# The last pairs of three graph layers in a drain of their own, in a four-layer graph network on one core

## The chip, the core and the metric

The kernel runs on one core of one Trainium2 chip. The metric is the device time of one execution in microseconds, lower is better; all matrix work is in fp32.

## The reference, cut to what matters

The input `x` holds 32 graphs of 512 nodes with 64 features; `adj` is one normalised 512 x 512 adjacency for all of them. Four layers follow each other, each with a layer norm before it and a residual around it:

```python
h = relu(layernorm(x)); x = x + (h @ w_self + adj @ h @ w_nbr + bias)      # layer 0
h = relu(layernorm(x)); z = h
for i in range(2): z = relu((adj @ z) @ weights[i])
x = x + z                                                                  # layer 1
h = relu(layernorm(x)); Wh = h @ W.T
e = leaky_relu(Wh @ a[:64] [:, None] + Wh @ a[64:] [None, :], 0.2)
x = x + elu(softmax(where(adj > 0, e, -9e15)) @ Wh)                        # layer 2
h = relu(layernorm(x)); ...                                                # layer 3
```

Layer 3 ("flow") is an attention over the graph with 8 heads of 128 features, followed by an output attention; its scores are products of the node features with themselves.

## The kernel before, in words

Graphs are worked on in pairs, 16 in all (`M`), two graphs side by side in 128 features. The first three layers form one software pipeline of slots: in slot `k`, `slot(k, more)` issues layer 0 of pair `k`, the norm of layer 1 for pair `k - 1`, the first half of layer 1 for pair `k - 2`, its second half for `k - 3`, and of layer 2 the preparation of pair `k - 4` and the attention of pair `k - 5`. There are `M + 5` slots, 0 to 20; in the last ones ever less of the pipeline is left. The order on TensorE, VectorE and ScalarE is the order in which the code issues, written out by hand; the queues of the engines are fed in that order, and a framework puts in the semaphores.

Layer 2 of a pair is an object of class `Gat`. Its steps, with the line numbers of the profile before:

- `flip` transposes the normed pair on TensorE and copies it on ScalarE (L290, L292).
- `prepare` computes the projected features `wh_ps` (L878) and one score vector `e1` (L885) on TensorE, then exponentials of the two score vectors on ScalarE (L894 to L897).
- `weigh` multiplies the features by those exponentials on VectorE (L902).
- `scores(part)` builds four of eight mask products `s` on VectorE (L911). A row of the softmax is the maximum of two exponentials times the mask.
- `values` multiplies the mask products by the weighted features on TensorE: 64 matmuls (128 records) into two PSUM accumulators `acc` (L924). The pool of accumulators holds one pair.
- `end` divides by the softmax sum on VectorE (L935, L936), which reads the accumulators; takes an exponential on ScalarE (L941); adds both parts to `x` (L944, L945); and centres the result and squares it for the norm of layer 3 (L773 to L775, L947).

`Norm.a` centres a pair (L773 to L775), `Norm.square` squares it on ScalarE, `Spread` sums variances (L811), takes the root on ScalarE (L818) and the reciprocal on VectorE (L826), and `Norm.relu` scales (L797). `neighbours` is a product with the adjacency (four matmuls, L833) and `project` one with a weight (L852).

`more` is one extra piece of work in a slot, issued after the slot's last neighbour product and ahead of `u.end()`. In slots 16 to 19 it is `judge_rows(c)` (L195 to L204), which checks a quarter of the adjacency's rows on VectorE; in slot 20 it is `judge` (L221 to L225), which reduces the checks to one flag: a reduction on VectorE, a transpose `own_ps` on TensorE, and two small VectorE steps on that. The flag is used at the end of the whole kernel.

In slot 19 pair 14 is `u` and pair 15 is `last`; both are ended there. Slot 20 takes the variances of what is left.

The flow stage follows under `planned`, which issues units of work by a fixed table of offsets. Its lead-in, `flow_slot(i)` for `i` from -12 to -2, is issued after slot 17. It makes the first graph's flow features: a norm on VectorE (L474 to L478), a scaling on GpSimd (`hs`, L483), a transpose on TensorE (`hx_ps`, L290), a copy, and the products `g_ps` (L508). The first scores `s_ps` (L386) and their VectorE step (L372) come after the pipeline has ended. SBUF buffers rotate: the pool `work_a` has two buffers of each name, `row_pair` 11 in all, `ps_a` four PSUM banks under one tag.

Of the kernel before, what the change touches and what calls it, by code (L numbers as in the profile page):

```python
# [8 lines left out]
F32 = mybir.dt.float32  # L9
AF = mybir.ActivationFunctionType  # L10
# [12 lines left out]
def fast_form(  # L23
# [731 lines left out]
    with (  # L755
# [105 lines left out]
        class Gat:  # L861
# [51 lines left out]
                        mask_t[b // C][:, b % C], op0=OP.max, op1=OP.mult,  # L913
                    )

            def values(self):

                self.acc = [
                    ps_g.tile([P, C, F + 1], F32, name="acc") for k in range(2)
                ]  # L920
                for r in range(C):
                    for b in range(2 * C):
                        for k in range(2):
                            nc.tensor.matmul(  # L924
                                self.acc[k][:, r],
                                lhsT=self.s[b // 2][halves(k), b % 2, r * P : (r + 1) * P],
                                rhs=self.v[halves(k), b],
                                start=(b == 0), stop=(b == 2 * C - 1),
                            )

            def end(self):
                rec = tiny.tile([P, 2, C], F32, name="rec")
                self.sq = o = work.tile([P, 2, C, F], F32, name="o")
                for k in range(2):
                    nc.vector.reciprocal(rec[:, k], self.acc[k][:, :, F])  # L935
                    nc.vector.tensor_tensor(  # L936
                        o[:, k], self.acc[k][:, :, :F],
                        rec[:, k, :, None].to_broadcast([P, C, F]), OP.mult,
                    )
                e = row_pair("e")[:, 0].rearrange("p (k c f) -> p k c f", k=2, c=C)  # L940
                nc.scalar.activation(e, o, AF.Exp)  # L941

                x4 = pair_of(self.i)
                nc.vector.scalar_tensor_tensor(x4, o, 0.0, x4, op0=OP.max, op1=OP.add)  # L944
                nc.vector.scalar_tensor_tensor(x4, e, 1.0, x4, op0=OP.min, op1=OP.add)  # L945
                self.mean = centre(o, self.i)
                nc.scalar.activation(o, o, AF.Square)  # L947
                ended.append(self)
# [12 lines left out]
        def start():  # L961
# [8 lines left out]
            order_adj()  # L970
            transpose_adj(ps_t)

        def slot(k, more):
# [25 lines left out]
            u = gat.pop(k - 5, None)  # L999
            if u:  # L1000
                u.scores(0)
            if k - 3 in nt1b:

                po = project([(nt1b.pop(k - 3), wl2[1])], "po1b")
                x4 = pair_of(k - 3)
                for i in range(2):
                    nc.vector.scalar_tensor_tensor(
                        x4[:, i], po[:, :, i, :], 0.0, x4[:, i], op0=OP.max, op1=OP.add
                    )
# [12 lines left out]
            if k - 4 in gat:  # L1022
                gat[k - 4].prepare()
            if l1:
                po = project([(nt1, wl2[0])], "po1a")
                z = work.tile([P, C, F2], F32, name="z")
                nc.scalar.activation(z, po.rearrange("p c b f -> p c (b f)"), AF.Relu)
# [12 lines left out]
            s.root()  # L1040
            if k - 4 in gat:
                gat[k - 4].weigh()
            s.turn()
            for n in some:
                if isinstance(n, Gat):
                    flow_stats[n.i] = n.mean, n.rstd
                else:
                    n.relu()
            if l0:
                po0[k] = project([(ht0, ws2), (nt0, wn2)], "po0")  # L1050
            if l1:
                nt1b[k - 2] = neighbours(lambda c: z[:, c, :])
            if more:
                more()

            last = gat.pop(M - 1) if k - 4 == M - 1 else None
            if last:
                last.scores(0)
                last.scores(1)
            if u:  # L1060
                u.end()
            if last:
                last.values()
                last.end()


        mask_t = [
# [14 lines left out]
        with tc.manual_schedule(  # L1082
            engines={
                mybir.EngineType.PE,
                mybir.EngineType.DVE,
                mybir.EngineType.Activation,
            }
        ):
            start()
            begun = {  # L1090
                0: gat_weights,
                1: edges,
                2: masks,
                3: flow_weights,
                4: scales,
                M + 4: judge,
            }
# [593 lines left out]
```

## Time and profile before

| what | value |
|---|---|
| median of 3 runs | 2339.39 us (2338.75 to 2340.38) |
| profiled execution | 2340.76 us |
| its span in the trace | 2338.9 us |
| TensorE, VectorE, ScalarE busy | 2248.0, 1794.3, 1576.3 us |
| one full slot of the pipeline | 24.37 us |
| in it TensorE, VectorE, ScalarE busy | 24.37, 20.75, 10.43 us |
| products of slot 15 begin | 338.21 us |
| first flow scores on TensorE, first step on them on VectorE | 459.83, 461.95 us |

All times of the trace are from the span's start. A row of the timeline has a start, a length, the engine, the line, the operation, what it writes and reads, the shapes and the number of records; in brackets stands the time for which the engine was idle ahead of it and who released it. TensorE's weight loads have an engine name of their own (PEld) and overlap the matmuls. A 512-column fp32 matmul is two records in the profile.

### The profile page before, as it was taken

The page shows a single profiled execution, that of the slowest core. Times are in us where ns is not written, and L with a number is a line of the kernel's source. Part 1 is how long each engine was busy: PE and PEld are TensorE (multiplying, and loading weights), DVE is VectorE, ACT ScalarE, POOL GpSimd, SP SyncE. Part 2 cuts the span into 40 slices and gives each one's busy share as a digit, 9 for nine tenths or more (in the row PEclk, how much of TensorE's full clock was granted, in tenths as well). Part 3 has the DMA queues.
Part 4 walks back from the last instruction along what each step waited for, and adds up shares of the span by engine and source line. Part 5 has one row for each costly group of instructions (what it writes and reads, how often), then busy time and mean ns, then how long its engine had stood idle before and what let it go on. Part 6 is the DMA issues. An engine that isn't in the chain of part 4 may idle for free.

```text
span 2338.9 us, 49561 instructions
## 1 busy us (share of the span) xinstructions
PE 2248.0 (96%) x19066; PEld 1086.8 (46%) x19066; DVE 1794.3 (77%) x4366; ACT 1576.3 (67%) x3674; POOL 68.4 (3%) x104
## 2 busy tenths in 40 slices
PE   7999998799999999999999999999999999999997
PEld 4676776644444444444444444444444444444443
DVE  6788878677878787878787878787878787878776
ACT  3444433287777777777777777677777777877775
POOL 2000000000000000000000000000000000000000
PEclk9999999599999999999999999999999999999999
DMA  4000000000001000000000000000000000000001
GB/s 125 1 1 1 2 1 1 1 24 20 29 20 29 20 29 19 29 20 29 20 28 20 29 20 29 19 29 20 29 20 28 20 29 20 24 20 24 24 20 39
DMA packets 44645, 53.11 MB, mean 23 GB/s; under 512 B 15928, under 2 KB 25312, under 8 KB 44272
## 3 DMA queue, kind: packets, MB, share of 16 engines
q1 hardware_dynamic: 43888, 49.65, 6.9%
q8 instruction: 152, 2.49, 0.5%
q14 instruction: 93, 0.76, 0.1%
q0 software_dynamic: 512, 0.20, 0.1%
HBM read 43.98 MB, written 4.78 MB: 21 GB/s over the span
## 4 chain that ended last, share of the span: by engine, by line
PE 72%; DVE 4%; POOL 2%; issue 1%; ACT 0%; DMA 0%; SPq 0%; POOLq 0%; DVEq 0%
PE s_ps L386 23%; PE av L414 23%; PE pt_ps L399 13%; PE y_ps L526 5%; PE gT_ps L565 5%; PE g_ps L508 2%; DVE pt_att L407 2%; POOL hs L483 2%; PE hx_ps L290 1%; DVE hn L475 1%; DVE s_att L372 1%; DVE hn L474 0%; DVE gs L583 0%; PE gV_ps L576 0%; PE back_ps L449 0%
## 5 line engine op out<-in xcount | busy, mean ns | idle before, releaser
L365 ACT ACTIVATE p_att<-s_att,negmax 128x512 f32<-128x512 f32 x1152 | 827.7, 723 | 0.0
L372 DVE CUSTOM_DVE_ANT_0 s_att<-s_ps,flow_neg 128x512 f32<-128x512 f32 x1152 | 739.5, 679 | 2.4 <-PE s_ps L386 2.1
L407 DVE COPY pt_att<-pt_ps 128x512 f32<-128x512 f32 x576 | 395.5, 687 | 281.2 <-PE pt_ps L399 226.6
L386 PE MATMUL s_ps<-hx,g 64*128 64x512 f32 x2048 | 570.0, 634 | 5.7 <-DVE negmax L372 5.1
L414 PE MATMUL av<-pt_att,hn 128*64 128x512 f32 x2048 | 552.3, 618 | 0.0
L399 PEld LDWEIGHTS pt_ps<-ident,p_att 64*128 64x128 f32 x9216 | 373.6, 138 | 375.0 <-issue 228.0
L405 ACT COPY pt_att<-pt_ps 128x512 f32<-128x512 f32 x576 | 335.3, 582 | 157.9 <-PE pt_ps L399 152.2
L399 PE MATMUL pt_ps<-ident,p_att 64*128 64x64 f32 x9216 | 415.6, 226 | 2.8 <-DVE pt_att L407 0.9
L534 ACT ACTIVATE cat<-y_ps,bh 128x512 f32<-128x512 f32 x256 | 162.2, 684 | 168.4 <-PE y_ps L526 168.4
L386 PEld LDWEIGHTS s_ps<-hx,g 64*128 64x128 f32 x2048 | 156.1, 187 | 243.6 <-DVE negmax L372 180.6
L365 ACT ACTIVATION_READ_ACCUMULATOR p_att<-s_att,negmax 128x1 f32 x1152 | 224.6, 195 | 0.0
L443 DVE TENSOR_TENSOR o_att<-av,recb 128x512 f32<-128x512 f32 x144 | 99.6, 692 | 140.5 <-PE av L414 139.1
L414 PEld LDWEIGHTS av<-pt_att,hn 128*64 128x64 f32 x2048 | 101.2, 134 | 156.8 <-PE s_ps L386 87.2
L311 DVE SCALAR_TENSOR_TENSOR cat<-cat 128x1024 f32<-128x1024 f32 x128 | 155.5, 1215 | 0.0
L924 PE MATMUL acc<-v,s 64*128 64x65 f32 x2048 | 132.5, 291 | 1.5 <-DVE rec L935 0.8
L924 PEld LDWEIGHTS acc<-v,s 64*128 64x128 f32 x2048 | 129.5, 206 | 6.9 <-issue 2.6
L565 PE MATMUL gT_ps<-cat,wo_sb 128*64 128x512 f32 x512 | 131.7, 593 | 0.0
L526 PE MATMUL y_ps<-o_att,wh_sb 64*128 64x512 f32 x512 | 131.6, 591 | 0.0
L520 ACT COPY g<-g_ps 128x512 f32<-128x512 f32 x128 | 68.8, 589 | 84.2 <-PE g_ps L508 84.2
L833 PE MATMUL nt_ps<-adj_t,hn 128*128 128x512 f32 x256 | 116.2, 597 | 0.8 <-DVE hn L797 0.8
L386 PE MATMUL s_ps<-gs 64*128 64x512 f32 x256 | 72.4, 642 | 24.2 <-DVE gs L583 24.2
L372 DVE DVE_READ_ACCUMULATOR2_ANT negmax<- 128x1 f32 x1152 | 95.3, 83 | 0.0
(166 smaller groups left out, 1571.7 us busy)
## 6 DMA issues: line engine op xcount, KB each, us to landing
recb<-rec_row SPq DMA_DIRECT2D x288, 128.0 KB
rec_row<-rect SPq DMA_DIRECT2D x576, 1.0 KB
out_dram<-y SPq DMA_DIRECT2D x32, 128.0 KB
x<-in_x_dram SPq DMA_DIRECT2D x3, 1024.0 KB
x<-in_x_dram SPq DMA_DIRECT2D x4, 256.0 KB
adj_raw<-in_adj_dram SPq DMA_DIRECT2D x1, 1024.0 KB
mask<-mask SPq DMA_DIRECT2D x4, 256.0 KB
wh_sb<-in_L_gnn_Wh_dram SPq DMA_DIRECT2D x2, 256.0 KB
```

Of the source, the lines that this page charges most:

```text
L311: nc.vector.scalar_tensor_tensor(t, t, 0.01, t, op0=OP.mult, op1=OP.max)
L365: nc.scalar.activation(self.p[:, k, r, :], ns[:, k], AF.Exp, bias=self.negmax[:, k, r : r + 1], scale=-1.0, accum_out=self.sum[:, k, r : r ...
L372: nc.vector.tensor_tensor_reduce(out=ns[:, k], in0=ps[:, k], in1=flow_neg[:, r], scale=-1.0, scalar=BIG, op0=OP.add, op1=OP.min, accum_out ...
L386: nc.tensor.matmul(ps[:, k], lhsT=g[halves(k), r * P : (r + 1) * P], rhs=x[halves(k), :], start=True, stop=True,)
L399: nc.tensor.transpose(ps[half][:, k, r], self.p[halves(half), k, r, j * P : (j + 1) * P], ident[halves(half), halves(half)],)
L405: nc.scalar.copy(pth[:, :, :, 0, :], ps[0])
L407: return lambda: nc.vector.tensor_copy(pth[:, :, :, 1, :], ps[1])
L414: nc.tensor.matmul(self.av[halves(k), :], lhsT=self.v(k, j), rhs=pt[k], start=(j == 0), stop=(j == C - 1),)
L526: nc.tensor.matmul(ps, lhsT=wh_sb[halves(k), h, :], rhs=self.o[halves(k), :], start=True, stop=True,)
L534: nc.scalar.activation(self.cat[:, k], pss[k], AF.Identity, bias=bh[:, h : h + 1], scale=1.0)
L565: nc.tensor.matmul(self.gps[halves(k), :], lhsT=wo_sb[:, h, :], rhs=Heads.cat[b + k, h], start=(h == 0), stop=(h == H - 1),)
L924: nc.tensor.matmul(self.acc[k][:, r], lhsT=self.s[b // 2][halves(k), b % 2, r * P : (r + 1) * P], rhs=self.v[halves(k), b], start=(b == 0) ...
```

## The change

Slots run only to 16 (`range(M + 1)`). What remains of the pipeline is issued by a new function, `drain`, in an order of its own. `Gat.end` is split into `read`, which reads the accumulators, and `rest`; `Gat.values` can be issued in parts. A new function `fill(n)` issues `n` products of the adjacency with the identity whose result nobody reads. The row checks move from slots 16 to 19 to slots 6, 8, 10 and 12, and `judge` from slot 20 to slot 15. The flow's lead-in moves from behind slot 17 to a place ahead of the last pair's products.

The diff, cut: the second half of layer 1 and its first half become functions `ends` and `middle` with the same statements, and the code for `last` in `slot` goes.

```diff
-            def values(self):
+            def values(self, rows=range(C)):
...
-                for r in range(C):
+                if 0 in rows:
+                    self.acc = [
+                        ps_g.tile([P, C, F + 1], F32, name="acc") for k in range(2)
+                    ]
+                for r in rows:
...
             def end(self):
+                self.read()
+                self.rest()
+
+            def read(self):
                 rec = tiny.tile([P, 2, C], F32, name="rec")
...
+            def rest(self):
+                o = self.sq
                 e = row_pair("e")[:, 0].rearrange("p (k c f) -> p k c f", k=2, c=C)
                 nc.scalar.activation(e, o, AF.Exp)
...
+        def fill(n):
+            p = ps_t.tile([P, N], F32, name="fill_ps", tag="ps")
+            for i in range(n):
+                nc.tensor.matmul(p, lhsT=ident, rhs=adj_t[:, 0, :], start=True, stop=True)
+
+        def drain():
+            g2, g1, g0 = gat.pop(M - 4), Gat(M - 3, n2.pop(M - 3).h), None
+            nt1b[M - 2] = copied(nt1b[M - 2], "nt1b")
+            h = n1.pop(M - 1).h
+            nt1 = copied(neighbours(lambda c: h[:, c]), "nt1")
+            g1.flip()
+            g2.scores(0)
+            ends(M - 2)
+            n = make(n2, M - 2)
+            n.a()
+            n.square()
+            g2.scores(1)
+            z = middle(nt1)
+            g1.prepare()
+            nt1b[M - 1] = neighbours(lambda c: z[:, c, :])
+            s = Spread()
+            s.add(n)
+            u = ended.pop()
+            s.add(u)
+            s.root()
+            nt1b[M - 1] = copied(nt1b[M - 1], "nt1b")
+            g2.values(range(C // 2))
+            g1.weigh()
+            s.turn()
+            n.relu()
+            flow_stats[u.i] = u.mean, u.rstd
+            g0 = Gat(M - 2, n2.pop(M - 2).h)
+            ends(M - 1)
+            n = make(n2, M - 1)
+            n.a()
+            n.square()
+            g2.values(range(C // 2, C))
+            g1.scores(0)
+            g0.flip()
+            g2.read()
+            g1.scores(1)
+            g0.prepare()
+            fill(3)
+            s = Spread()
+            s.add(n)
+            s.root()
+            g1.values()
+            s.turn()
+            n.relu()
+            last = Gat(M - 1, n2.pop(M - 1).h)
+            last.flip()
+            g0.weigh()
+            g2.rest()
+            g0.scores(0)
+            g1.read()
+            last.prepare()
+            g0.scores(1)
+            fill(3)
+            g0.values()
+            last.weigh()
+            g1.rest()
+            last.scores(0)
+            s = Spread()
+            s.add(g2)
+            for i in range(-3 * C, -1):
+                flow_slot(i)
+            g0.read()
+            last.scores(1)
+            fill(3)
+            last.values()
+            g0.rest()
+            s.add(g1)
+            last.read()
+            last.rest()
+            fill(6)
+            s.add(g0)
+            s.add(last)
+            s.root()
+            s.turn()
+            for n in (g2, g1, g0, last):
+                flow_stats[n.i] = n.mean, n.rstd
...
-                M + 4: judge,
             }
             for c in range(C):
-                begun[M + c] = lambda c=c: judge_rows(c)
-            for k in range(M + 5):
+                begun[6 + 2 * c] = lambda c=c: judge_rows(c)
+            begun[7 + 2 * C] = judge
+            for k in range(M + 1):
                 slot(k, begun.get(k))
-                if k == M + 1:
-                    for i in range(-3 * C, -1):
-                        flow_slot(i)
+            drain()
```

In `drain`, `g2`, `g1`, `g0` and `last` are layer 2 of pairs 12, 13, 14 and 15; `C` is 4.

More of the change, by code (lines that the diff above doesn't have):

```diff
@@ L914, in scores @@
                     )
-            def values(self):
-                self.acc = [
-                    ps_g.tile([P, C, F + 1], F32, name="acc") for k in range(2)
-                ]
-                for r in range(C):
+            def values(self, rows=range(C)):
[4 more added lines that the diff above has]
+                for r in rows:
                     for b in range(2 * C):
@@ L971, in start, with ends, middle @@
             transpose_adj(ps_t)
+        def ends(i):
+            po = project([(nt1b.pop(i), wl2[1])], "po1b")
+            x4 = pair_of(i)
+            for k in range(2):
+                nc.vector.scalar_tensor_tensor(
+                    x4[:, k], po[:, :, k, :], 0.0, x4[:, k], op0=OP.max, op1=OP.add
+                )
+        def middle(nt1):
+            po = project([(nt1, wl2[0])], "po1a")
+            z = work.tile([P, C, F2], F32, name="z")
+            nc.scalar.activation(z, po.rearrange("p c b f -> p c (b f)"), AF.Relu)
+            return z
         def slot(k, more):
@@ L1002, in slot @@
             if k - 3 in nt1b:
[L1004 to L1009, printed above, removed]
+                ends(k - 3)
             if l0:
@@ L1024, in slot @@
             if l1:
-                po = project([(nt1, wl2[0])], "po1a")
-                z = work.tile([P, C, F2], F32, name="z")
-                nc.scalar.activation(z, po.rearrange("p c b f -> p c (b f)"), AF.Relu)
+                z = middle(nt1)
             n = make(n0, k + 1)
@@ L1054, in slot @@
                 more()
[L1056 to L1059, printed above, removed]
             if u:
                 u.end()
-            if last:
-                last.values()
-                last.end()
+        def fill(n):
+            p = ps_t.tile([P, N], F32, name="fill_ps", tag="ps")
+            for i in range(n):
+                nc.tensor.matmul(p, lhsT=ident, rhs=adj_t[:, 0, :], start=True, stop=True)
@@ new lines, in drain @@
+        def drain():
[10 more added lines that the diff above has]
+            g2.scores(1)
+            z = middle(nt1)
+            g1.prepare()
[61 more added lines that the diff above has]
+                flow_stats[n.i] = n.mean, n.rstd
```

## The prediction

> **What bounds the kernel now.** I first read the 40 slices of the page: TensorE's row is at 9 nearly everywhere and its granted clock at 9, except in one slice.
>
> ```profile
> PE   7999998799999999999999999999999999999997
> PEclk9999999599999999999999999999999999999999
> ```
>
> Slice 8 (409 to 468 us) holds the end of the first three layers. Apart from the moved row checks and verdict, the change touches only what lies from 375 us to the flow's start, so this is where it can win. Next I read TensorE's timeline there (start, length, work, and in brackets how long TensorE stood and for whom):
>
> ```profile
> 386.66 3.70 PE L833 MATMUL nt_ps<-adj_t,z 128*128 128x512 f32 x8
> 394.53 1.03 PE L290 MATMUL hx_ps<-ident,hs 128*128 128x128 f32 x4 [4.17 <-POOL hs L483]
> ...
> 405.28 7.71 PE L924 MATMUL acc<-v,s 64*128 64x65 f32 x128
> 412.92 0.66 PE L290 MATMUL ht_ps<-ident,hn 128*128 128x128 f32 x4
> 419.48 2.00 PE L878 MATMUL wh_ps<-wgv,ht 64*64 64x65 f32 x32 [5.91 <-ACT ht L292]
> 421.27 1.92 PE L885 MATMUL e_ps<-ht,wa 64*64 64x512 f32 x4
> 423.12 13.92 PE L924 MATMUL acc<-v,s 64*128 64x65 f32 x128
> 437.85 14.43 PE L924 MATMUL acc<-v,s 64*128 64x65 f32 x128 [0.82 <-DVE rec L935]
> 459.00 0.37 PE L223 MATMUL own_ps<-ident,own 128*1 128x128 f32 x1 [6.72 <-DVE own L221]
> ```
>
> The 128 product records of a pair (L924) take 7.71 us at 405 us and 13.92 and 14.43 us later: TensorE stands three times (4.17, 5.91, 6.72 us) and then runs at half its clock. A table of stages (length, busy time and count of PE, PEld, DVE, ACT, POOL, granted clock, DMA) gives the clock:
>
> ```profile
> 394.53:404.88 10.35, 9.08 (x56) 5.66 (x56) 4.51 (x9) 3.01 (x6) 0.00 (x0) 0.51 0.01 2
> 404.88:415.12 10.24, 8.57 (x134) 7.72 (x132) 9.93 (x22) 4.02 (x10) 0.00 (x0) 1.00 0.01 2
> 415.12:437.85 22.73, 17.55 (x164) 15.78 (x165) 19.48 (x35) 5.64 (x11) 0.00 (x0) 0.50 0.00 1
> 437.85:452.30 14.45, 14.43 (x128) 14.19 (x128) 3.67 (x8) 1.26 (x2) 0.00 (x0) 0.50 0.01 1
> ```
>
> VectorE is the other bound: it feeds the mask products (L911) and reads the accumulators (L935). Its first flow instruction (L372) starts at 461.95; I count the gain to that point, as the flow after it repeats one pattern.
>
> [...] the clock changes near 394.6, 404.9, 415.1 and 462.9 us[...]. And 29 us of products at half clock (423.1 to 452.3) did not restore it, while 3.1 us of 512-column score products (L386 from 459.83) did.
> [...]
> [...]
>
> **The change part by part.** Prices are steps from start to start in the timelines: one mask product 0.66; reading a pair's accumulators 1.2 (368.90 to 370.12); the rest of a pair's end 3.05 (370.12 to 373.17); centring 1.5; variance 0.6; weighing 0.66; a neighbour product of four 3.43; `prepare` 1.94; a 128-column projection 0.9 to 1.1; a pair's products 7.3 at full clock; a fill 0.86 (a quarter of 3.43). The compiled order of the changed kernel gives the sequence on each engine.
>
> *Row checks* (`judge_rows`, 4.03 us of VectorE each, 383.60 to 387.62) move from slots 16 to 19 into 6, 8, 10, 12. There TensorE is busy for all of a 24.37 us slot and VectorE for 20.75, so 3.6 us are idle (3.26 of them just where the checks land). The half microsecond left over is absorbed in the next slot. Cost 0. Were the cover gone, 4 x 4 us. In the drain they stood beside half-clock products; the part that they cost there is contained in the sum.
>
> *The verdict* (`judge`) moves from the very end into slot 15. At the end it cost about 1 us (458.84 to 459.83). In slot 15, L224 waits for `own_ps`, which TensorE issues behind slot 15's neighbour products: 350.82 + 0.37 = 351.2; with L224 and L225 (0.28, 0.14) VectorE goes on at 351.65, where before it read the accumulators at 345.60. All behind it is 6.0 us late: slot 16's last mask product ends at 351.65 + 14.2 = 365.9 (before 345.60 to 360.76, with 0.93 of waiting), and TensorE, which needs 5.7 more after it, finishes slot 16 at 371.65 instead of 366.63. **5.0 us are lost here**; only TensorE's wait hides the remainder.
>
> *The drain.* From 371.65: neighbour products to 375.1, `nt1` 378.5, flip and projection 379.85, middle and prepare 382.85, a 0.6 wait for z behind ScalarE's square, second neighbour products 386.9, pair 12's two halves with the projection of pair 15 between them 395.1. VectorE: read 12's predecessor at 371.7, two mask groups with pair 14's norm to 384.85, variance and weighing to 387.8, waits 3.75 for that projection, pair 15's norm 393.85, first masks of pair 13 396.5, read pair 12 397.7, second masks 400.35, norm and weighing 402.9, first add of pair 12's rest 403.6. TensorE: flip, copy, prepare, three fills to 400.7, pair 13's products to 408.0.
> Here is a new wait. On ScalarE the exponential of pair 12's rest (L949) stands behind the copy of pair 15's flip, and that flip stands behind pair 13's products: 408.0 + 0.45 + 0.6 for the copy + 1.28 for the table + 0.63 = 411.0. **VectorE stands 7.4 us** and with it pair 14's masks and the reading of pair 13: rest to 413.4, masks 416.05, read 417.25, last masks 419.9. TensorE has prepared and filled by 413.6, stands 3.7 us, and gets only 14 products (1.6 us) before 419.9. Over 6.3 us it is 26% busy, with products[...]. So I expect the clock to fall near 418.
> Then pair 14's products end at 431.3 instead of 425.6. The flow features (hn, hs of POOL, done near 429.8) are ready by then. Transposes 0.9, copy 0.6, `g_ps` 1.93 and three fills 5.14, all at half clock, would end at 439.9. These are 7.1 us of 512-column work[...]. Pair 15 products 446.1, read, rest, two variances: 451.9. The six fills end at 451.3 and the first scores at 452.2, so these fills cost nothing: VectorE is busy beside them.
> L372 starts at 452.2 instead of 461.95: **9.7 us gained**. No new DMA; the flow's lead-in issues the same POOL and SP work, later, with nobody waiting on SP.
>
> *Buffers.* `work` has two `o` tiles and ps_g one accumulator set; each is read before its successor is written in the walk. The 15 fills take PSUM slots whose readers are done by then.
>
> The profiled execution took 2340.76 us (span 2338.9 and 1.9 around it), 1.4 above the median of 2339.39. Taking the gain off the median: 2339.4 - 9.7 = 2329.7. About 0.2% (4.7 us) is what a measurement here can tell from no change.
>
> **Unknown costs, bounded.** (a) Slot 16 after the verdict: between 355.1 and 360.0 TensorE has only one projection (0.9 us). The clock may fall there; a 2.8 us hole at 79 us, beside full neighbour products, did not drop it. If it falls and the projections wake it: 2.5 us more; if products begin first and do not wake it: their 7.3 us doubled and some of the next group, about 9. Below zero is excluded: a slower clock helps nothing. I take 0 for the likeliest.[...]
>
> **The rivals.**
> 1. *The clock holds* through 413.6 to 419.9. Products of pair 14 end at 425.6, POOL's hs bounds the features (429.8), pair 15 ends at 441.7, L372 at 447.6: 14.3 gained, 2325.1. For it: the fills ahead. Against: 26% busy.
> 2. *Slot 16 falls to half clock and its products keep it there*: 9.7 - 9 = about 1 gained, 2339.
> 3. *Slower: fills do not wake the clock* after pair 14. Pair 15's products take 14.6 and end at 454.5, six fills 10.3 to 464.8, first scores 466.7, L372 at 466.8, 4.9 late, and the flow then starts with another 2 to 3 us at half clock: about 2346. It decides once the clock stays at half from 418 to the first scores. Against: 3.1 us of L386 woke it at 462.9. For: `g_ps` at 396.2 did not, though that was 1.7 us beside waits.
> 4. *The change doesn't do what it says*: flow features and fills sit in TensorE's order as named; what may fail is the clock, which is 3.
>
> **How the numbers follow.** Clock falls once and returns: 0.60 (in a third of it with 2.5 us of slot 16, 2332); holds: 0.14; slot 16 stuck: 0.12; fills fail: 0.14. Range 2324 to 2341: it takes in the first three and leaves the fourth out. Faster 0.73: the first two, less 0.01; same 0.13: rival 2 and that leak; slower 0.14: rival 3.
>
> **What would show it.** Right: VectorE waiting about 8.8 us for `own_ps` in slot 15; slot 16's products ending near 371.7; VectorE standing 7 us for the exponential of the rest while pair 13's products run; pair 14's products near 14 us and pair 15's near 7.3; L372 near 452. Wrong: no stall at the exponential; pair 15's products at 14 us (rival 3); all four pairs at 7.3 us (rival 1); steady slots longer than 24.37 us, which would mean that the row checks are not hidden.

## The result, and the profile after

The changed kernel takes **2331.79 us** (median of 9 runs, 2330.38 to 2332.94) beside 2340.38 us for the kernel before on the same chip (median of 9, 2337.22 to 2349.86). The ratio is 0.996, with a 95% interval of 0.9949 to 0.9972: 8.6 us faster, 2.1 us above the forecast time of 2329.7 and inside its range. The profiled execution has a span of 2331.1 us (before 2338.9). Busy times barely moved: TensorE 2250.7 us (before 2248.0, the 15 unread products included), VectorE 1792.3 (1794.3), ScalarE 1572.1 (1576.3). So no work was saved. What changed is how long TensorE stood, and how long it ran at half its clock; the page's slices show both.

```profile
PE   7999999899999999999999999999999999999997
PEclk9999999899999999999999999999999999999999
```

TensorE's row reads 9 and 8 where it read 8 and 7 before, and the one slice of the clock that read 5 (409 to 468 us before, 408 to 466 us here) reads 8: about half of the half clock of the drain is gone. Summed between 340 and 470 us from tables of 10 us stretches, TensorE is at half clock for 58.0 us before and 27.2 us after. How much of the gain hangs on that is a question for e4 below.

TensorE's timeline of the changed kernel, from slot 16 to the flow's start:

```profile
357.25 2.01 PE L852 MATMUL po1b<-wl,nt1b 128*128 128x128 f32 x8 [2.08 <-ACT nt1b L840]
...
365.00 7.36 PE L925 MATMUL acc<-v,s 64*128 64x65 f32 x128
...
402.72 7.36 PE L925 MATMUL acc<-v,s 64*128 64x65 f32 x128
...
413.33 2.84 PE L1078 MATMUL fill_ps<-adj_t,ident 128*128 128x512 f32 x6
418.91 14.46 PE L925 MATMUL acc<-v,s 64*128 64x65 f32 x128 [2.73 <-DVE o L941]
...
437.10 3.90 PE L1078 MATMUL fill_ps<-adj_t,ident 128*128 128x512 f32 x6
440.93 7.36 PE L925 MATMUL acc<-v,s 64*128 64x65 f32 x128
448.23 5.42 PE L1078 MATMUL fill_ps<-adj_t,ident 128*128 128x512 f32 x12
```

The lengths of equal work are the reading here. Pair 13's products (402.72) and pair 15's (440.93) take 7.36 us, where before the last two pairs took 13.92 and 14.43; pair 14's (418.91) still take 14.46. The eight records of `po1b` at 357.25 take 2.01 us instead of about 1.1: the clock had fallen in slot 16 too, and the products at 365.00 are back at full clock. In two-microsecond stretches the clock falls at 357.4 and rises at 364.2, falls at 418.8 and rises at 439.3: 6.8, 54.6 and 20.5 us apart.

VectorE's timeline of the changed kernel has the two new waits, and the end of the stage:

```profile
351.34 0.28 DVE L224 TENSOR_REDUCE unsound<-own_ps 1x1 f32<-1x128 f32 x1 [8.72 <-PE own_ps L223]
...
351.72 0.16 DVE L940 RECIPROCAL rec<-acc 128x4 f32<-128x4 f32 x1
...
413.32 0.69 DVE L953 SCALAR_TENSOR_TENSOR x<-e,x 128x512 f32<-128x512 f32 x1 [8.29 <-ACT e L949]
...
453.44 0.69 DVE L811 TENSOR_REDUCE var<-o 128x8 f32<-128x512 f32 x1 [0.16 <-ACT o L955]
454.96 0.69 DVE L372 CUSTOM_DVE_ANT_0 s_att<-s_ps,flow_neg 128x512 f32<-128x512 f32 x1 [0.83 <-PE s_ps L386]
```

VectorE stands 8.72 us for the verdict's transpose (L224) and 8.29 us for the exponential of pair 12's rest (L949). The first flow step (L372) starts at 454.96 instead of 461.95. What precedes slot 15 and what follows L372 is the same: slot 15's products begin at 338.41 (before 338.21), and from L372 to the end of the span it is 1876.1 us (before 1877.0).

The end of this stretch has changed too. In the kernel before, the verdict stood between the last variance (L811) and the first flow step:

```profile
457.05 0.69 DVE L811 TENSOR_REDUCE var<-o 128x8 f32<-128x512 f32 x1 [0.16 <-ACT o L947]
...
459.41 0.28 DVE L224 TENSOR_REDUCE unsound<-own_ps 1x1 f32<-1x128 f32 x1 [0.47 <-PE own_ps L223]
...
461.95 0.69 DVE L372 CUSTOM_DVE_ANT_0 s_att<-s_ps,flow_neg 128x512 f32<-128x512 f32 x1 [2.09 <-PE s_ps L386]
```

From the end of that variance to L372 it is 4.2 us before and 0.8 us after. From the start of slot 15's products to L372 the changed kernel is 7.2 us shorter; 3.4 us of them come from this end, and 3.8 us from what lies ahead of it.

### The profile page after: what moved, and what is told of

It reads as the page before. It is cut to its first block, busy times and chain, and to the rows that moved or that the text cites. A ratio compares the mean times of both kernels' runs of the same rounds, so it can differ in the third digit from the quotient of the medians.

```text
span 2331.1 us, 49615 instructions
## 1 busy us (share of the span) xinstructions
PE 2250.7 (97%) x19096; PEld 1083.9 (46%) x19096; DVE 1792.3 (77%) x4365; ACT 1572.1 (67%) x3671; POOL 67.9 (3%) x104
## 4 chain that ended last, share of the span: by engine, by line
PE 90%; DVE 5%; POOL 2%; issue 1%; ACT 1%; DMA 0%; SPq 0%; POOLq 0%; DVEq 0%; ACTq 0%
PE s_ps L386 23%; PE av L414 23%; PE pt_ps L399 13%; PE nt_ps L833 7%; PE acc L925 5%; PE y_ps L526 5%; PE gT_ps L565 5%; PE g_ps L508 2%; DVE pt_att L407 2%; POOL hs L483 2%; PE po L852 1%; PE hx_ps L290 1%; PE po1a L852 1%; PE wh_ps L878 1%; PE ht_ps L290 1%
## 5 line engine op out<-in xcount | busy, mean ns | idle before, releaser
L372 DVE CUSTOM_DVE_ANT_0 s_att<-s_ps,flow_neg 128x512 f32<-128x512 f32 x1152 | 739.5, 679 | 0.9 <-PE s_ps L386 0.8
L925 PE MATMUL acc<-v,s 64*128 64x65 f32 x2048 | 125.1, 282 | 2.7 <-DVE o L941 2.7
L925 PEld LDWEIGHTS acc<-v,s 64*128 64x128 f32 x2048 | 122.7, 197 | 7.5 <-DVE o L941 3.6
L372 DVE DVE_READ_ACCUMULATOR2_ANT negmax<- 128x1 f32 x1152 | 95.1, 83 | 0.0
```

What stands on the lines that cost most here:

```text
L372: nc.vector.tensor_tensor_reduce(out=ns[:, k], in0=ps[:, k], in1=flow_neg[:, r], scale=-1.0, scalar=BIG, op0=OP.add, op1=OP.min, accum_out ...
L925: nc.tensor.matmul(self.acc[k][:, r], lhsT=self.s[b // 2][halves(k), b % 2, r * P : (r + 1) * P], rhs=self.v[halves(k), b], start=(b == 0) ...
```

## The experiments

The useful measure beside the median is **the stage**: the time from the start of slot 15's products to the first L372 in the profiled execution. It leaves out what differs ahead of slot 15. The last column is worked out as the difference of the two medians of each comparison, on one chip.

| kernel | stage us | median us | ratio to before (95%) | us to before |
|---|---|---|---|---|
| before | 123.74 | 2340.38 | 1 | 0 |
| after | 116.55 | 2331.79 | 0.9960 (0.9949 to 0.9972) | -8.6 |
| e1 verdict later | 111.57 | 2328.19 | 0.9950 (0.9936 to 0.9963) | -12.0 |
| e2 exponential first | 104.27 | 2321.93 | 0.9920 (0.9906 to 0.9933) | -18.2 |
| e3 both | 98.74 | 2314.24 | 0.9889 (0.9873 to 0.9904) | -25.9 |
| e4 after, no fills | 116.35 | 2333.33 | 0.9969 (0.9957 to 0.9981) | -6.8 |
| e5 before, rows moved | 120.64 | 2334.96 | 0.9971 (0.9958 to 0.9984) | -6.6 |
| e6 after, four more fills | 115.18 | 2331.59 | 0.9958 (0.9943 to 0.9973) | -9.9 |
| e7 before, with fills | 111.02 | 2331.60 | 0.9953 (0.9936 to 0.9971) | -9.9 |
| e8 both, no fills | 102.12 | 2321.20 | 0.9910 (0.9891 to 0.9928) | -20.3 |
| e9 checks in the drain | 114.45 | 2332.22 | 0.9959 (0.9947 to 0.9972) | -8.7 |
| e10 before, rows and fills | 115.68 | 2330.71 | 0.9956 (0.9943 to 0.9968) | -10.2 |
| e11 after, once more | 115.93 | 2331.50 | 0.9959 (0.9946 to 0.9971) | -9.4 |
| e12 both, fills elsewhere | 101.97 | 2315.08 | 0.9884 (0.9866 to 0.9902) | -25.8 |

The theory under test is the prediction's: the old drain lost its time to the half clock, the new one wins most of that back and gives part of it away to two new waits on VectorE. The rivals are that the fills, the removed row checks or the mere order carry the gain, or that the waits are hidden. Each expectation below says which theories it tells apart.

### The two new waits: e1, e2, e3

e1 issues the verdict later, in the drain, beside pair 15's second half of layer 1:

```diff
             g0 = Gat(M - 2, n2.pop(M - 2).h)
+            judge()
             ends(M - 1)
...
-            begun[7 + 2 * C] = judge
```

> The changed kernel with the verdict (judge) moved from slot 15 to the drain, ahead of ends(M - 1), where VectorE waits 4.35 us for TensorE anyway. Theory A (two in-order queues and the clock): VectorE no longer stands 8.7 us in slot 15, slot 16 ends 5 us earlier, and the clock does not fall there (2 us more): 6 to 7.5 us below the changed kernel's 2331.8, so 2324.5 to 2326. Theory B (the gain is VectorE's relief from the row checks; waits are covered): within 1 us of 2331.8, since the verdict is one short reduction. Theory C (the fills carry the gain): no change either, as the fills stay.

Measured: 2328.19 us, stage 111.57. On VectorE's timeline of e1 the verdict's wait has shrunk, and it lies where VectorE waits for TensorE anyway (4.35 us for `po1b` in the changed kernel):

```profile
386.01 0.28 DVE L224 TENSOR_REDUCE unsound<-own_ps 1x1 f32<-1x128 f32 x1 [3.39 <-PE own_ps L223]
```

On its TensorE timeline slot 16 keeps the full clock (the same eight records of `po1b` that took 2.01 us):

```profile
354.25 1.06 PE L852 MATMUL po1b<-wl,nt1b 128*128 128x128 f32 x8
```

The stage is 5.0 us shorter than after's (116.55 - 111.57). The median fell by 3.4 us, each against its own before (12.0 less 8.6; 2.6 with e11's 9.4), and the two intervals overlap. That is less than the 6 to 7.5 us that were expected: the 2 us that the expectation put on slot 16's half clock don't show, not even in the stage. The clock still falls ahead of pair 14's products, for as long as in the changed kernel: by the tables of 10 us stretches both are at half clock for 20.4 us there. So the verdict in slot 15 costs 5 us of the stage and some 3 us of the medians.

e2 leaves the verdict and issues pair 15's flip behind pair 12's rest, so that on ScalarE the exponential no longer stands behind the copy of that flip:

```diff
-            last.flip()
             g0.weigh()
             g2.rest()
+            last.flip()
```

> The changed kernel with g0.weigh() and g2.rest() issued ahead of last.flip(), so that on ScalarE the exponential of pair 12 stands ahead of the copy that waits for pair 13's products. Theory A: VectorE's stall of 8.3 us goes, pair 14's masks and pair 13's reading are in time, pair 14's products run at full clock (7.4 us instead of 14.5), and the flow starts some 12 us earlier: 2319 to 2321. Theory B: VectorE has idle time elsewhere in the drain and the stall is hidden: within 2 us of 2331.8. Theory C: at most the 5.6 us between the products and the fills, none if the clock still falls.

Measured: 2321.93 us, 0.9 above theory A's range; stage 104.27, 12.3 us shorter than after's. ScalarE's timeline says why. After, in the changed kernel:

```profile
410.76 0.59 ACT L292 COPY ht<-ht_ps 128x512 f32<-128x512 f32 x1 [8.02 <-PE ht_ps L290]
411.36 1.28 ACT L949 ACT_TABLE_LOAD   x1
412.65 0.63 ACT L949 ACTIVATE e<-o 128x512 f32<-128x512 f32 x1
```

and in e2:

```profile
402.80 1.28 ACT L949 ACT_TABLE_LOAD   x1
404.09 0.63 ACT L949 ACTIVATE e<-o 128x512 f32<-128x512 f32 x1
410.79 0.59 ACT L292 COPY ht<-ht_ps 128x512 f32<-128x512 f32 x1 [2.60 <-PE ht_ps L290]
```

The copy ends at the same time in both; the exponential runs 8.6 us earlier, since it needs only VectorE's `o`, which had long been there. With it VectorE reads pair 13 in time, and on e2's TensorE timeline the next pair follows its fills without a hole and at full clock:

```profile
413.37 2.84 PE L1078 MATMUL fill_ps<-adj_t,ident 128*128 128x512 f32 x6
416.14 7.36 PE L925 MATMUL acc<-v,s 64*128 64x65 f32 x128
```

So one small instruction behind a copy cost the changed kernel about 10 us by the medians (-18.2 against -8.6): part as the wait of VectorE, part as the clock that TensorE lost in the hole which this wait opened. No run parts the two.

e3 has both edits.

> The edits of e1 and e2 together. Theory A: the two costs lie one after the other, so they add: 12 + 6.5 = 18.5 us below the changed kernel, 2312 to 2315, with the clock full until the flow. If they share a wait: 2317 to 2320. Theories B and C: within 3 us of 2331.8.

Measured: **2314.24 us** (2313.02 to 2315.32), ratio 0.9889 (0.9873 to 0.9904), stage 98.74. The tables of 10 us stretches from 340 to 470 us show no half clock any more (granted 1.00 in each). The stage is 25.0 us shorter than before's, of which the change itself brought 7.2. This is the best version that repeats: 1.1% below the kernel before and, by the two ratios, some 0.7% below the changed one.

### What the fills are worth: e4, e6, e8

e4 is the changed kernel without any `fill`; e8 is e3 without any.

```diff
-            fill(3)
...
-            fill(6)
```

> The changed kernel without its four fills (15 unread products). Theory C: the clock falls ahead of pair 13's products already and stays down to the flow; pair 15's products take 14.5 us and the gain is gone: 2338 to 2346. Theory A: the fall near 419 is not prevented by the fills anyway; what they do is wake the clock ahead of pair 15's products. Without them pair 13's products stay at full clock, pair 15's run at half (7 us more), less the 3.9 us that the third fill takes: 2 to 5 us above 2331.8, so 2334 to 2337. Theory B: no change, 2331 to 2333.

Measured: 2333.33 us, a little below theory A's range, just above theory B's and far from theory C's; stage 116.35. The fills of the changed kernel are worth 1.8 us by the medians against their own before, which the intervals don't separate from nothing, and nothing by the stage. e4's TensorE timeline shows two pairs at half clock instead of one, but with nothing in between:

```profile
420.48 14.43 PE L925 MATMUL acc<-v,s 64*128 64x65 f32 x128 [5.61 <-DVE rec L940]
...
438.50 13.76 PE L925 MATMUL acc<-v,s 64*128 64x65 f32 x128
452.05 3.73 PE L386 MATMUL s_ps<-hx,g 64*128 64x512 f32 x8
```

Pair 15's products cost 6.4 us more there (13.76 against 7.36), and the flow's first scores 1.74 more (3.73 against 1.99), but pair 15's products begin 5.9 us earlier, counted from slot 15 (438.50 - 341.90 against 440.93 - 338.41), since no fills stand ahead of them. What the fills win in clock they take up themselves.

This run also says how much of the change's gain hangs on the clock: little. By the same tables e4 is at half clock for 51.2 us, nearly as long as the kernel before (58.0), and its stage is as short as after's. In the stage TensorE is busy for 103.4 us before, 101.5 in e4 and 107.8 after, and idle for 20.3, 14.8 and 8.8 us. What e4 shares with the changed kernel is the new order, the moved verdict and the moved row checks (worth 3.1 us of the stage in the old order, e5). One thing that the new order removes stands on ScalarE. Before, the copy of pair 15's flip was issued behind the square of pair 13's end, which waits for VectorE:

```profile
418.32 0.63 ACT L947 ACTIVATE o<-o 128x512 f32<-128x512 f32 x1 [2.61 <-DVE o L775]
418.86 0.57 ACT L292 COPY ht<-ht_ps 128x512 f32<-128x512 f32 x1
```

TensorE stood 5.91 us for this copy, and after the change it stands 0.73 us for it:

```profile
411.40 1.15 PE L878 MATMUL wh_ps<-wgv,ht 64*64 64x65 f32 x32 [0.73 <-ACT ht L292]
```

Another 4.1 us are gone at the end of the stage, where e4's L372 follows the last variance after 0.15 us. How the 7.4 us of e4's stage divide between these places no run shows.

> e3 (verdict later, exponential first) without any fill. If the fills are needed only because of the stalls: TensorE has no wait left that is long enough, and the time stays within 1 us of e3. If they are needed all the same: the clock falls once between pairs 13 and 15 and costs 4 to 8 us over e3 (up to 18 where it does not come back).

Measured: 2321.20 us, stage 102.12, against 2314.24 and 98.74 with fills: 5.6 us by the medians against their own before, whose intervals overlap a little, 4.0 by the spans (2317.4 and 2313.4), 3.4 by the stage. e8's TensorE timeline has the hole that the fills close: the transposes of the flow features wait 3.22 us for GpSimd's scaling, and the clock falls (granted 0.50 from 420 to 430 us).

```profile
416.80 0.74 PE L290 MATMUL hx_ps<-ident,hs 128*128 128x128 f32 x4 [3.22 <-POOL hs L483]
...
420.09 13.76 PE L925 MATMUL acc<-v,s 64*128 64x65 f32 x128
```

With both waits gone the fills save 3.4 us of the stage; with the waits in place they save none.

e6 tries the opposite in the changed kernel: four more fills where TensorE stood 2.73 us ahead of pair 14's products.

```diff
             g0.scores(1)
-            fill(3)
+            fill(7)
             g0.values()
```

> The changed kernel with 7 instead of 3 fills ahead of pair 14's products, 3.4 us more of unread products where TensorE stands 2.7 us. If the clock falls for the idle time alone: it holds, pair 14's products take 7.4 us instead of 14.5, and the flow starts 4 to 6 us earlier, 2326 to 2328. If the thin stretch of products that wait for their masks also counts: the clock still falls, but later and is woken earlier, 2 to 3 us less, 2329 to 2330. Theory B: 0 to 1 us more, 2332 to 2333.

Measured: 2331.59 us, stage 115.18: 1.4 us better in the stage, nothing that the medians can tell. The time lies above both of the ranges that were expected for a clock that holds or wakes earlier, and a little below theory B's. e6's TensorE timeline:

```profile
421.70 5.80 PE L925 MATMUL acc<-v,s 64*128 64x65 f32 x100 [0.22 <-DVE s L911]
430.72 1.11 PE L290 MATMUL hx_ps<-ident,hs 128*128 128x128 f32 x4 [3.22 <-POOL hs L483]
```

Pair 14's products are at full clock and end 5.9 us earlier (427.5 against 433.4). TensorE then stands 3.22 us for `hs`, which comes out of VectorE's norm, and the clock falls in that hole: transposes and fills run at half clock as before (1.11 and 5.02 us, where e2 has 0.66 and 2.84 at full clock). So the half clock of pair 14's products was mostly hidden: of the 5.9 us, 3.2 go into the wait for `hs`.

### The kernel before, with parts of the change: e5, e7, e10

e5 is the kernel before with the row checks moved, e7 with 26 fills where its TensorE stood, e10 with both.

```diff
-                begun[M + c] = lambda c=c: judge_rows(c)
+                begun[6 + 2 * c] = lambda c=c: judge_rows(c)
```

> The kernel before with nothing but the row checks moved to slots 6, 8, 10 and 12; the verdict stays at the end. Theory B (the gain is VectorE's relief): most of the 8.6 us, 2331 to 2334. Theory A: slots 6 to 12 stay at 24.37 us, TensorE's three waits remain and so does the half clock; 0 to 4 us below before, 2336 to 2340.

Measured: 2334.96 us, between the ranges of the two theories; stage 120.64. The medians say 6.6 us, the stage 3.1. The 12 runs form two groups, six from 2330.97 to 2333.41 us and six from 2336.51 to 2339.79, and the median lies in the gap between them. The profile is of a run at 2337.72, so the stage belongs to the slower group; that run is 3.8 us below the median before, close to the stage's 3.1. Either way the checks cost something where they stood in the old order.

```diff
                 gat[k - 4].flip()
+                if k == M + 3:
+                    fill(7)
...
+            if k == M + 4:
+                fill(8)
             if more:
                 more()
...
             if last:
+                fill(6)
                 last.values()
...
                 if k == M + 1:
+                    fill(5)
                     for i in range(-3 * C, -1):
                         flow_slot(i)
```

> The kernel before, its order kept, with unread products alone: 5 ahead of the flow's lead-in, 7 between flip and prepare in slot 19, 6 ahead of pair 15's products, 8 at the head of slot 20. Theory A (the half clock is what the drain cost): TensorE keeps or soon regains its clock, the products of pairs 14 and 15 take 7.4 us instead of 13.9 and 14.4, and the time falls by 9 to 15 us, 2325 to 2331, with no new order at all. Theory of order (the sequence in the drain matters, the clock follows from it): VectorE bounds the old order, the extra products only fill its waits, and 0 to 4 us are won.

Measured: 2331.60 us, 0.6 above theory A's range, with the profile of a 2326.96 us execution: stage 111.02, no half clock in the same tables (1.00 in each). Its TensorE timeline:

```profile
410.31 6.17 PE L976 MATMUL fill_ps<-adj_t,ident 128*128 128x512 f32 x14
...
420.48 5.80 PE L924 MATMUL acc<-v,s 64*128 64x65 f32 x100 [0.22 <-DVE s L911]
...
431.76 7.87 PE L924 MATMUL acc<-v,s 64*128 64x65 f32 x128
```

In the old order and with nothing else changed, 26 products whose result nobody reads win 12.7 us of the stage where the clock holds, and 9.9 us in the median. So the half clock cost the old drain at least these 12.7 us. That the new order gains by its clock doesn't follow from this, and e4 speaks against it. Two of the six runs are near 2327 us with a mean granted clock of 0.998, four near 2332 with 0.995 to 0.996.

> The kernel before with the row checks moved to slots 6 to 12 (e5) and the unread products of e7, old order otherwise. If the two act on different terms (VectorE's work, TensorE's clock) they add: 6.5 + 9.9 = 16.4 us below before, 2323 to 2326. If both remove the same half-clock time, the sum is that of the larger, 2329 to 2332. What then still separates it from e3 (25.9 us below before) is the worth of the order alone.

Measured: 2330.71 us, -10.2 us where the two parts alone would add up to 16.5; that is the expectation's second case. e10's TensorE timeline shows one pair at half clock again, the one ahead of the fills:

```profile
404.66 10.10 PE L924 MATMUL acc<-v,s 64*128 64x65 f32 x100 [0.22 <-DVE s L911]
415.60 8.00 PE L976 MATMUL fill_ps<-adj_t,ident 128*128 128x512 f32 x14
```

A hundred records that take 5.80 us at full clock take 10.10. e7 has the same records, behind the same pieces of work on TensorE, at full clock:

```profile
404.08 5.80 PE L924 MATMUL acc<-v,s 64*128 64x65 f32 x100 [0.22 <-DVE s L911]
```

So old order, rows and fills together reach 2330.7 us, and the new order with its two waits mended 2314.2. The difference of some 15 us isn't the order alone: e10 also has 13.6 us at half clock and 11 unread products more than e3. The profiles of e7 and e3, both without half clock, are 12.3 us of the stage apart; that is the new order together with the moved checks, the moved verdict and 11 unread products fewer.

### Where the checks should stand, and a repeat: e9, e11, e12

e9 is the changed kernel with all checks in the drain, `judge_rows(0)` in slot 16 and the other three and the verdict further on:

```diff
+            judge_rows(1)
...
             ends(M - 1)
...
+            judge_rows(2)
             last = Gat(M - 1, n2.pop(M - 1).h)
...
+            judge_rows(3)
             g0.read()
...
             s.turn()
+            judge()
...
-                begun[6 + 2 * c] = lambda c=c: judge_rows(c)
-            begun[7 + 2 * C] = judge
+                if c == 0:
+                    begun[M] = lambda: judge_rows(0)
```

> The changed kernel with the row checks put back late: one in slot 16 as before, three in the drain where VectorE stood in the changed kernel (ahead of pair 15's projection, 4.35 us; ahead of the exponential, 8.3 us; ahead of reading pair 14, 2.8 us); the verdict goes to the very end. Theory A: they fit into those waits, so moving them early bought nothing in this order; the time is that of e1, where the verdict no longer stops slot 15, or up to 3 us more: 2326 to 2331. Theory B (VectorE's relief from 16 us is the gain): 6 to 12 us more, 2334 to 2341.

Measured: 2332.22 us, between the ranges of the two theories; stage 114.45, 2.1 us shorter than after's where the verdict's removal alone was worth 5.0 (e1). The other 3 us lie at the end of the stage, where the verdict is back between the last variance and the first flow step:

```profile
451.28 0.69 DVE L811 TENSOR_REDUCE var<-o 128x8 f32<-128x512 f32 x1 [0.16 <-ACT o L955]
...
456.28 0.69 DVE L372 CUSTOM_DVE_ANT_0 s_att<-s_ps,flow_neg 128x512 f32<-128x512 f32 x1 [2.09 <-PE s_ps L386]
```

From the end of that variance to L372 it is 4.3 us, and 0.8 in e1. From slot 15's products to the end of the variance e9 takes 110.1 us and e1 110.7, so the row checks cost next to nothing in the new drain: pair 14's products begin 0.7 us later than e1's, counted from slot 15, and an earlier return of the clock makes that good (the fills ahead of pair 15's products take 3.42 us, in e1 4.69). The checks run where VectorE waits: its wait at L953 is 4.26 us instead of 8.29, with `judge_rows(2)` in what was waiting time. VectorE is busy for 91.6 us of e9's stage, as before the change (92.0; after 75.6), so its relief from them is not what the changed kernel gains by.

> The changed kernel as it is, beside the others on one chip, for the size of the difference to e1 (12.0 us below before in its own comparison, 8.6 here so far). Theory A: 7 to 10 us below before.

Measured: 2331.50 us, 0.9959 (0.9946 to 0.9971): measured again, the same kernel gives the same gain. In its profile the clock falls at the same two places, in slot 16 later than after (`po1b` at full clock in 1.16 us instead of 2.01, `wh_ps` behind it at half clock in 2.00 us), and the stage is 115.93.

e12 takes e8 and puts fills in two places only:

```diff
+            fill(4)
             for i in range(-3 * C, -1):
                 flow_slot(i)
...
             last.rest()
+            fill(6)
```

> e3 with other fills: none ahead of the products of pairs 13, 14 and 15, four ahead of the flow features where TensorE stands 3.2 us for GpSimd in e8, and the six at the end. If fills cost time where TensorE has no long wait and pay only where it has one: the clock stays full, pair 15's products begin 2 to 3 us earlier than in e3, 1 to 4 us below e3: 2310 to 2313. If the clock needs the earlier fills: it falls at pair 14 and the time is that of e8, 2319 to 2322.

Measured: 2315.08 us, but as two groups, one for each of the expected cases: 2310.11, 2311.03 and 2311.40 us with granted clocks of 0.998 to 0.999, and 2318.75, 2319.37 and 2320.39 with 0.994 to 0.995. The profile is of one of the second group, and its TensorE timeline has pair 14 at half clock:

```profile
408.47 10.94 PE L925 MATMUL acc<-v,s 64*128 64x65 f32 x100 [0.22 <-DVE s L911]
```

Ahead of these records TensorE works off the first ones of the pair as VectorE delivers their masks. e8, whose code is the same up to here, has the same stretch of work and keeps its clock:

```profile
407.78 5.80 PE L925 MATMUL acc<-v,s 64*128 64x65 f32 x100 [0.22 <-DVE s L911]
```

So the work alone doesn't decide whether the clock survives that stretch. That the faster group of e12 is the one in which it does is likely, but no profile is of that group. e12's better half beats e3 by some 3 us, its worse half loses 5; the medians don't tell the two apart.

## Why the prediction was right, point by point

- **The size.** Near, and a little lucky. From slot 15's products to L372 the forecast gained 9.7 us and the profiles 7.2. The medians give 8.6, mainly because the nine runs of the kernel before have a median 1.0 us above that of the three which the forecast started from.
- **What bounds it.** Half right. The half clock was a loss of the old drain: e7 wins it back in the old order with fills alone. But what the changed kernel gains doesn't hang on it. e4 has 51.2 us of half clock and the same stage as the changed kernel. The profiles show two other places where time went: TensorE no longer stands 5.91 us for a copy, and the verdict has left the end of the stage. How the gain divides between them stays open.
- **Row checks at no cost in slots 6 to 12.** Right: slot 15's products begin 0.2 us later than before (338.41 and 338.21), after four moved checks. In the new drain they would have cost next to nothing either (e9).
- **The verdict loses 5.0 us.** Right in mechanism and size: VectorE goes on at 351.72 (forecast 351.65) after a wait of 8.72 us (8.8), and e1 gains 5.0 us of the stage. What it cost at its old place is undersized: the forecast says about 1 us, and from the last variance to L372 the profiles have 4.2 us before, 4.3 in e9 and 0.8 after. That end also holds the root of the variances.
- **Unknown (a), slot 16's clock, taken as nothing.** The clock did fall there, at 357.4, and rose at 364.2. Between 354.0 and the fall TensorE worked for about 1.2 us (to 355.17) and then stood 2.08 us for `nt1b`. It cost 0.7 us, as slot 16's products ended at 372.36 (forecast 371.65), and not the 2.5 us that the forecast estimated for this case. That its sum for the case, 2332, is what was measured is luck.
- **Where the 2.8 us come from** by which L372 is late (454.96 against 452.2). No single step has them: 0.7 us in slot 16, 0.9 more up to the end of pair 12's products (396.69 against 395.1), 0.7 more up to the exponential, and the remainder behind pair 15's products.
- **The new wait at the exponential.** Right in place and cause: 8.29 us against 7.4, ending at 413.3 against 411.0. TensorE then stood 2.73 us with the clock falling at 418.8 (forecast near 418). Between 415.4 and 418.8 it worked for 0.8 us. What the forecast's step rests on holds in this trace: ScalarE takes the exponential behind the copy that was issued ahead of it (412.65 and 410.76), and the `ACT_TABLE_LOAD` between them takes 1.28 us, as in the profile before (408.68, L941). The forecast had this wait and the fall in its sum. That it was the dearest thing in the changed kernel, and could be had back by moving one line, is what e2 adds.
- **Clock back in the features and fills.** Right. Where in this work the clock returns was the author's estimate, which the trace before doesn't show; the forecast's sum lets pair 15's products begin at 438.8 (446.1 less 7.3). Measured are 439.3 for the clock and 440.93 for the products, each behind the lateness of the exponential. Transposes, `g_ps` and fills are 1.11, 2.08 and 3.90 us; pair 15's products are at full clock, 7.36 us against 7.3.
- **The six last fills cost nothing.** Nearly: TensorE ended them at 453.65 and VectorE its last variance at 454.13, but the first scores stand behind the fills, and VectorE waits 0.83 us for them at L372.
- **Rival 1, the clock holds** (2325.1). Its place was wrong: e6 kept the clock through pair 14's products and came to 2331.59, because TensorE then stood 3.22 us for `hs` and the clock fell one step later. The sum of that rival contained the wait for `hs` but not that it would cost the clock.
- **Rival 2, products hold slot 16 at half clock.** Not what happened: the clock came back at 364.2, behind `wh_ps` and `e_ps` (2.00 and 1.92 us, from 360.05), 0.8 us ahead of the products.
- **Rival 3, fills don't wake the clock** (2346). Not what happened; the clock came back in the fills ahead of pair 15. In e4, without any fills, pair 15's products take 13.76 us, and it still came to 2333.33; it does not carry the fills' own time at half clock, which the sum of that rival contained.
- **Two readings of the clock.** That the clock would fall in a stretch 26% busy was the author's estimate. At the fall before, at 415.1, TensorE had worked for 1.8 us since 411.7, 1.3 of them products and the others transposes. And the hole of 2.80 us at 79 us, which the forecast has as one that did not drop the clock, did drop it in other executions, as the next paragraphs show.

Three times the same stretch of work on TensorE kept the clock in one execution and lost it in another: the records of e7 and e10, those of e8 and e12, and the hole of 2.80 us ahead of `urow_ps` (L187) at 79 us, which all 14 profiles have. Twelve of them pass it at full clock. In e4 and e9 the clock falls at 81.7 and stays down for about 7 us, and the eight records of `urow_ps` take 2.04 us instead of 1.13. That is 3.0 of the some 3.6 us by which these two profiles reach slot 15 later than the profile before (341.90 and 341.83 against 338.21).

In the changed kernel 2.08 us of standing in slot 16 and 2.73 us ahead of pair 14, each beside little work, were enough for the clock to fall. What decides a fall stays open. Ahead of it TensorE had stood for 4.8 us in e4 (414.9 to 419.7). In e10 and e12 it had stood for no more than 0.23 us at a time, in the 7 us up to 405.6 and in the nearly 5 us up to 408.4, and the work just ahead was products with 65 columns. With the clock down, 14.46 us of such products (from 418.91) did not bring it back; it rose after some 4 us of 512-column work (`g_ps` and the first fills, 435.09 to 439.3). Whether the 65 columns make the difference isn't shown: no run varies the shape alone.

Why e5's runs form two groups is left unexplained.

## What to carry to other kernels

ScalarE and VectorE worked in the order of issue here: the exponential ran 8.6 us earlier once it was issued ahead of the copy (e2), and the reading of the accumulators waited behind the verdict until 351.72. So ask of each small instruction what stands ahead of it: a copy that waits for TensorE ahead of an exponential, and a reduction that waits for a transpose ahead of a reading, gave away some 17 us here, twice what the whole change had won. Price a wait with the clock that it takes along: in the changed kernel TensorE lost it at waits of 2.08 and 2.73 us, in e10 and e12 with none over 0.23 us just ahead. A fallen clock isn't yet a loss, though: e4 keeps nearly all of the old half clock and gains as much as the changed kernel does in the stage. Products that nobody reads paid here only where the work behind them really ran faster and nothing else was late; take the waits out first, then add them (3.4 us of the stage in e3 against e8, none in the changed kernel against e4).

## What the runs showed of the hardware that was not expected

- A hole of about 2 us beside one short group of work was enough to drop the clock in slot 16 (2.08 us at 355.2, the fall at 357.4), while e1, with no such hole, kept it (`po1b` in 1.06 us).
- The same hole of 2.80 us, with the same work around it, dropped the clock in two of 14 executions and not in the other twelve (79 us; e4 and e9).
- The clock fell among products of 65 columns, with no hole over 0.22 us in the 7 us ahead of the fall (e10, at 405.6).
- Executions of one and the same kernel form two groups some 8.7 us apart (e12: 2310.8 and 2319.5 on average, worked out from three runs each), with granted clocks of 0.998 to 0.999 and 0.994 to 0.995, and less widely in e7 (near 2327 and 2332 us). A median of few runs of such a kernel says little.
